# Loading the first batch first, keeping the tensor engine warm, and sampling the scores between projections, in a fused attention kernel

## The chip, the cores and the metric

The kernel runs on one core of a Trainium2 chip. A core has a tensor engine for matrix products (PE in the profile, with its weight loads listed as PEld), a vector engine (DVE), a scalar engine (ACT), a general-purpose engine (POOL) and a synchronising engine (SP) that here only starts transfers. Each engine works through its own list of instructions in order and waits on semaphores for the others. The metric is the device time of one execution in microseconds (us); the smaller the better. The kernel before takes 2685.39 us, the median of three runs that lie between 2684.89 and 2687.76.

## The reference

Four batches of an image of 128 channels and 64 x 64 = 4096 positions go through a group normalisation and an attention over positions with 64-wide queries and keys, then through a causal attention over the same 4096 tokens, then through a recurrent layer. Cut to what matters here:

```python
# layer 0: group norm over groups of 4 channels and all positions, then full attention
xn = _gn(x)                                   # mean and variance of 4 channels x 4096 positions
q = einsum('oc,bcn->bon', Wq, xn) + bq        # 64 wide
k = einsum('oc,bcn->bon', Wk, xn) + bk        # 64 wide
v = einsum('oc,bcn->bon', Wv, xn) + bv        # 128 wide
probs = softmax(einsum('bci,bcj->bij', q, k)) # 4096 x 4096 for each batch
x = x + einsum('bcj,bij->bci', v, probs)
# layer 1: layer norm over channels, causal attention, residual
t = t + causal_attention(_ln_t(t), Wq, Wk, Wv)
# then a layer norm, a product with W, a batch norm over all tokens,
# and a recurrence y = sigmoid(wx_t + y @ V.T) over positions, residual
```

Nothing of the attention of a batch can start before the statistics of that whole batch are known, because the normalised input feeds every projection.

## The kernel before

Only the parts that the change and the prediction touch are shown; `...` marks cuts. `P` is 128, `QT` is 512, `N` is 4096, `NQ` is 8, `B` is 4, `CQ` is 64.

The loads stand first. The input goes into one on-chip tile `X` by eight transfers of half a batch each, started by SP; all weights and biases are started by ACT. The transfers of both engines share a small set of completion semaphores in turn, so a transfer late in the list waits for an earlier one that used the same semaphore, whichever engine started that.

```python
    X = xpool.tile([P, B, N], F32, name="X")
    for b in range(B):
        for h in range(2):
            cols = ts(h, N // 2)
            nc.sync.dma_start(out=X[:, b, cols], in_=x[b, :, cols])        # L91
    def load(src, shape, name):
        t = const.tile(shape, F32, name=name)
        nc.scalar.dma_start(out=t, in_=src)
        return t
    ...
    for h in range(2):
        nc.scalar.dma_start(out=W0k[:, h, :], in_=w0k)
        nc.scalar.dma_start(out=W0q[:, h, :], in_=w0q)
        nc.scalar.dma_start(out=B0k[ds(h * CQ, CQ), :], in_=b0k)
        nc.scalar.dma_start(out=B0q[ds(h * CQ, CQ), :], in_=b0q)
    W0v = load(w0v, [P, C], "W0v")
    ...                                        # B0v, W1q, W1k, W1v, FW, FV, Fgamma, Fbeta
```

Then constants (`ident`, `same`, `ones`, `group`, `mask`, `blocks`). Before any work on the batches, the query and key weights of layer 1 are folded into one matrix:

```python
        for n, w in (("q", W1q), ("k", W1k)):
            pw = ps_m.tile([P, P], F32, tag="m", name=f"pw_{n}")
            nc.tensor.transpose(pw, w, ident)                              # L210
            wt[n] = tmp.tile([P, P], F32, tag="wt", name=f"wt_{n}")
            nc.vector.tensor_copy(wt[n], pw)                               # L212
        pa = ps_m.tile([P, P], F32, tag="m", name="pa")
        nc.tensor.matmul(pa, lhsT=wt["q"], rhs=wt["k"], start=True, stop=True)   # L214
        nc.vector.tensor_scalar(A1, pa, float(C) ** -0.5, None, ALU.mult)        # L216
```

The work on a batch is a set of jobs, each a generator whose steps are put between the steps of the attention. `ps_m` has two buffers (tag "m") and serves all the small products. The group norm scales the weights rather than the input:

```python
        def groupnorm(b):
            for c in range(NQ):
                nc.vector.bn_stats(stats[:, c, :], X[:, b, ts(c, QT)])     # L260
                if c % 2:
                    yield
            nc.vector.bn_aggr(mv, stats...)                                # L264
            nc.tensor.matmul(pg, lhsT=gmat, rhs=mv, ...)                   # L267
            nc.vector.tensor_copy(gmv, pg)
            ...                                     # dev = (mean - group mean) squared
            yield
            nc.tensor.matmul(pd, lhsT=gmat, rhs=dev, ...)                  # L275
            ...                                     # gmv += pd; grs = (var + eps) ** -0.5 on POOL
            yield
            for n, w in (("k", W0k), ("v", W0v), ("q", W0q)):
                nc.vector.tensor_scalar(got[n], src, grs, None, ALU.mult)  # L284
            yield
            for i, n in enumerate("kvq"):
                nc.tensor.matmul(pb[:, i : i + 1], lhsT=got[n], rhs=gmv[:, 0:1], ...)   # L288
            ...                                     # biases bk, bv, bq
            for c in range(NQ):
                feeds[b].append(queue(feed0(b, c)))
                if c == 0:
                    preps[0, b, 0] = queue(prep0(b, 0))
        def feed0(b, c):                            # keys and values of 512 positions
            nc.tensor.matmul(pk, lhsT=gn[b]["k"], rhs=src, ...)            # L308
            nc.scalar.activation(K[0, b][:, ts(c, QT)], pk, AF.Identity, bias=gn[b]["bk"])
            yield
            for j in range(4):
                nc.tensor.matmul(pv[:, j, :], lhsT=src[:, ts(j, P)], rhs=gn[b]["v"], ...)   # L313
            nc.scalar.copy(V[0, b][:, 4 * c : 4 * c + 4, :], pv)
            yield
        def prep0(b, c):                            # queries of 512 positions
            nc.tensor.matmul(pq, lhsT=gn[b]["q"], rhs=X[:, b, ts(c, QT)], ...)   # L319
            nc.scalar.activation(Q[0, b, c], pq, AF.Identity, bias=gn[b]["bq"])
            yield
            if c == 0:
                yield from sample(0, b)
        def sample(layer, b):                       # one shift for all exponentials of the batch
            nc.tensor.matmul(pz, lhsT=K[layer, b][rows, 0:P], rhs=Q[layer, b, 0][rows, :], ...)
            nc.vector.tensor_reduce(m1, pz, AX.X, ALU.max)
            yield
            nc.tensor.transpose(pm, m1, ident)
            nc.vector.tensor_reduce(m2, pm, AX.X, ALU.max)
            yield
            nc.tensor.matmul(px, lhsT=ones[0:1, :], rhs=m2, ...)
            nc.vector.tensor_scalar(t, px, -1.0, SHIFT, ALU.mult, ALU.add)
            yield
```

The attention itself runs over units of 256 keys by 512 queries: `score(i)` makes two score products (tile `ps`), adds the causal mask on the diagonal, and takes the exponential on ACT; `product(i)` multiplies it with the values (tile `av`) and adds it into a running total on DVE. Layer 0 has 8 x 16 units for each batch, layer 1 has 72. The scores of the next unit are issued ahead of the products of this one:

```python
        start_batch(0)                              # queues groupnorm(0)
        score(0)                                    # completes all feeds and the sample first
        for i in range(len(units)):
            if i + 1 < len(units):
                score(i + 1)
            turn()                                  # one step of each of the first two jobs
            product(i)
```

`product` calls `start_batch(b + 1)` at the first unit of the fourth query block of layer 1, so that the group norm of the next batch runs within layer 1 of this one. The order in which each engine finally holds its instructions is not that of the text alone: the recording layer moves an instruction forward where it sees its operands ready. In the kernel before, the 24 `bn_stats` of batches 1 to 3 stand on DVE at the very start of the program, among those of batch 0.

Of the kernel before, what the change touches and what calls it, by code (L numbers as in the profile page):

```python
# [26 lines left out]
F32 = mybir.dt.float32  # L27
AF = mybir.ActivationFunctionType
ALU = mybir.AluOpType
# [3 lines left out]
P = 128  # L33
QT = 512
# [30 lines left out]
def fast(  # L65
# [10 lines left out]
    nc = tc.nc  # L76
    B, C, N = x.shape
    CQ = w0q.shape[1]
    NQ = N // QT
# [4 lines left out]
    const = ctx.enter_context(tc.tile_pool(name="const", bufs=1))  # L84
    xpool = ctx.enter_context(tc.tile_pool(name="xres", bufs=1))

    X = xpool.tile([P, B, N], F32, name="X")
    for b in range(B):
        for h in range(2):
            cols = ts(h, N // 2)  # L90
            nc.sync.dma_start(out=X[:, b, cols], in_=x[b, :, cols])  # L91

    def load(src, shape, name):
        t = const.tile(shape, F32, name=name)
        nc.scalar.dma_start(out=t, in_=src)
        return t


    W0q = const.tile([P, 2, CQ], F32, name="W0q")
    W0k = const.tile([P, 2, CQ], F32, name="W0k")  # L100
    B0q = const.tile([P, 1], F32, name="B0q")
    B0k = const.tile([P, 1], F32, name="B0k")
    for h in range(2):
        nc.scalar.dma_start(out=W0k[:, h, :], in_=w0k)
        nc.scalar.dma_start(out=W0q[:, h, :], in_=w0q)
        nc.scalar.dma_start(out=B0k[ds(h * CQ, CQ), :], in_=b0k)
        nc.scalar.dma_start(out=B0q[ds(h * CQ, CQ), :], in_=b0q)
    W0v = load(w0v, [P, C], "W0v")
    B0v = load(b0v.rearrange("o c -> c o"), [P, 1], "B0v")
    W1q = load(w1q, [P, C], "W1q")  # L110
    W1k = load(w1k, [P, C], "W1k")
    W1v = load(w1v, [P, C], "W1v")
    FW = load(fw, [P, C], "FW")
    FV = load(fv, [P, C], "FV")
    Fgamma = load(fgamma, [P, 1], "Fgamma")
    Fbeta = load(fbeta, [P, 1], "Fbeta")


    ident = const.tile([P, P], F32, name="ident")
    make_identity(nc, ident)  # L120
    same = const.tile([P, R], F32, name="same")
    nc.vector.tensor_reduce(same, ident.rearrange("p (i r) -> p r i", r=R), AX.X, ALU.add)
    ones = const.tile([P, P], F32, name="ones")
    nc.gpsimd.memset(ones, 1.0)
    mhalf = const.tile([P, 4], F32, name="mhalf")
    nc.gpsimd.memset(mhalf, -0.5)
    group = const.tile([P, P // G, G], F32, name="group")
# [1 line left out]
    for base, sign in ((0, 1), (G - 1, -1)):  # L129
        nc.gpsimd.affine_select(  # L130
            out=group, in_=group, pattern=[[-sign * G, P // G], [0, G]], base=base,
# [6 lines left out]
        out=mask, in_=mask, pattern=[[1, P]], base=0,  # L138
# [13 lines left out]
    def rsqrt(dst, src, eps, n):  # L152

        nc.vector.tensor_scalar(dst, src, eps, None, ALU.add)  # L154
        nc.gpsimd.tensor_tensor(dst, dst, mhalf[:, :n], ALU.pow)  # L155
# [39 lines left out]
    with ExitStack() as actx:  # L195
# [3 lines left out]
        tmp = actx.enter_context(tc.tile_pool(name="tmp", bufs=2))  # L199
# [3 lines left out]
        ps_av = actx.enter_context(tc.tile_pool(name="ps_av", bufs=1, space=PSUM))  # L203
        ps_m = actx.enter_context(tc.tile_pool(name="ps_m", bufs=2, space=PSUM))


        wt = {}
        for n, w in (("q", W1q), ("k", W1k)):
            pw = ps_m.tile([P, P], F32, tag="m", name=f"pw_{n}")
            nc.tensor.transpose(pw, w, ident)  # L210
            wt[n] = tmp.tile([P, P], F32, tag="wt", name=f"wt_{n}")
            nc.vector.tensor_copy(wt[n], pw)  # L212
        pa = ps_m.tile([P, P], F32, tag="m", name="pa")
        nc.tensor.matmul(pa, lhsT=wt["q"], rhs=wt["k"], start=True, stop=True)  # L214
        A1 = const.tile([P, P], F32, name="A1")
        nc.vector.tensor_scalar(A1, pa, float(C) ** -0.5, None, ALU.mult)  # L216

        jobs = deque()

        def queue(steps):  # L220
            job = Job(steps)
            jobs.append(job)
            return job
# [8 lines left out]
        norms, ends, preps, feeds = {}, {}, {}, {}  # L232
# [23 lines left out]
        def groupnorm(b):  # L256

            stats = small.tile([P, NQ, 6], F32, tag="stats", name=f"stats_{b}")
            for c in range(NQ):
                nc.vector.bn_stats(stats[:, c, :], X[:, b, ts(c, QT)])  # L260
                if c % 2:
                    yield
            mv = small.tile([P, 2], F32, tag="mv", name=f"mv_{b}")
            nc.vector.bn_aggr(mv, stats.rearrange("p c s -> p (c s)"))  # L264
            gmat = group.rearrange("p a g -> p (a g)")
            pg = ps_m.tile([P, 2], F32, tag="m", name=f"pg_{b}")
            nc.tensor.matmul(pg, lhsT=gmat, rhs=mv, start=True, stop=True)  # L267
            gmv = small.tile([P, 2], F32, tag="gmv", name=f"gmv_{b}")
            nc.vector.tensor_copy(gmv, pg)
            dev = small.tile([P, 1], F32, tag="dev", name=f"dev_{b}")  # L270
            nc.vector.tensor_tensor(dev, mv[:, 0:1], gmv[:, 0:1], ALU.subtract)
            nc.vector.tensor_tensor(dev, dev, dev, ALU.mult)
            yield
            pd = ps_m.tile([P, 1], F32, tag="m", name=f"pd_{b}")
            nc.tensor.matmul(pd, lhsT=gmat, rhs=dev, start=True, stop=True)  # L275
            nc.vector.tensor_tensor(gmv[:, 1:2], pd, gmv[:, 1:2], ALU.add)
            grs = small.tile([P, 1], F32, tag="grs", name=f"grs_{b}")
            rsqrt(grs, gmv[:, 1:2], 1e-5, 1)
            yield
            got = {}  # L280
            for n, w in (("k", W0k), ("v", W0v), ("q", W0q)):
                src = w if n == "v" else w.rearrange("p h o -> p (h o)")
                got[n] = small.tile([P, P], F32, tag=f"w{n}", name=f"w{n}_{b}")
                nc.vector.tensor_scalar(got[n], src, grs, None, ALU.mult)  # L284
            yield
            pb = ps_m.tile([P, 3], F32, tag="m", name=f"pb_{b}")
            for i, n in enumerate("kvq"):
                nc.tensor.matmul(  # L288
                    pb[:, i : i + 1], lhsT=got[n], rhs=gmv[:, 0:1], start=True, stop=True
                )  # L290
            for i, (n, bias) in enumerate((("k", B0k), ("v", B0v), ("q", B0q))):
                got["b" + n] = small.tile([P, 1], F32, tag=f"b{n}", name=f"b{n}_{b}")
                nc.vector.tensor_tensor(got["b" + n], bias, pb[:, i : i + 1], ALU.subtract)
            gn[b] = got
# [5 lines that stand above are left out]
# [99 lines left out]
        for layer, b, c in tiles:  # L399
            n = 2 * (c + 1) if layer else N // (2 * P)  # L400
# [7 lines left out]
        def score(i):  # L408
            layer, b, c, u, n = units[i]
            t = layer, b, c  # L410
            if u == 0:
                if layer == 0 and c == 0:
                    for job in feeds[b]:
                        job.complete()
                if layer == 1:
                    ends[0, b, c].complete()
                    norms[b, c].complete()
                if t not in preps:
                    preps[t] = queue((prep1 if layer else prep0)(b, c))
                preps[t].complete()  # L420
                totals[t] = tot.tile([P, 2, QT], F32, tag="total", name=f"tot_{layer}_{b}_{c}")
            s = totals[t] if u == 0 else sp.tile([P, 2, QT], F32, tag="s", name=f"s_{i}")
            exps[i] = s
            first = [columns(layer, c, u, h) for h in range(2)]
            ps = ps_pair.tile([P, 2, QT], F32, tag="pair", name=f"ps_{i}")
            for h in range(2):
                rows = slice(0, P) if layer else ds(h * CQ, CQ)
                nc.tensor.matmul(  # L428
                    ps[:, h, first[h] :], lhsT=K[layer, b][rows, ts(2 * u + h, P)],
                    rhs=Q[t][rows, first[h] :], start=True, stop=True,  # L430
                )
            if layer and u >= 2 * c:
                for h in range(2):
                    edge = ps[:, h, ds(first[h], P)]
                    nc.vector.tensor_tensor(edge, edge, mask, ALU.add)  # L435
                if u == 0:
                    nc.gpsimd.memset(s[:, 1, : first[1]], 0.0)
            for a in [(slice(None), slice(0, QT))] if first[1] == 0 else [
                (h, slice(first[h], QT)) for h in range(2)
            ]:  # L440
                nc.scalar.activation(s[:, *a], ps[:, *a], AF.Exp, bias=shift[layer, b])  # L441
# [48 lines left out]
        def start_batch(b):  # L490
            feeds[b] = []
            feeds[b].append(queue(groupnorm(b)))

        start_batch(0)
        score(0)
        for i in range(len(units)):
            if i + 1 < len(units):
# [549 lines left out]
```

## Time and profile before

| what | value |
|---|---|
| time, median of 3 | 2685.39 us |
| span of the profiled execution | 2683.1 us |
| tensor engine busy | 97% of the span |
| vector engine busy | 56% |
| scalar engine busy | 42% |
| first half of batch 0 usable on DVE | 6.50 us |
| first matmul of any kind | 15.57 us |
| first key projection | 24.25 us |
| first exponential | 49.28 us |
| first product with the values | 50.45 us |

Times in the table from the fifth row on are starts, counted from the start of the span. To read the profile: the timeline lists merged instructions as start, busy time, engine, source line, operation, output and input tiles, shape and count, and in square brackets the idle time of the engine just before it with what ended it. The chain of waits goes back from the last instruction through whatever released each step, so its shares say which engine the end of the kernel hung on. One product of 128 x 512 values appears as two matmul records, and a record's busy time is modelled, so that times between starts say more than lengths.

### The profile page before, as it was taken

The numbers are of one execution on the slowest core, as the hardware profiler recorded it, in microseconds if no ns is written. First come the engines' busy times: TensorE is split into PE (matmuls) and PEld (weight loads), VectorE is DVE, ScalarE is ACT, GpSimd is POOL, SyncE is SP. The second block draws the span as 40 slices with busy tenths as digits, with TensorE's granted clock in tenths as the row PEclk, the third lists the DMA queues.
The fourth block names the chain that finished last, engine by engine and source line by source line (L and its number), as shares of the span: only waits on it lengthen the run. The fifth ranks groups of instructions, "written<-read, shape, count | busy, mean of one in ns | idle before, by whom it ended". The sixth has DMA issues, their size and how long they took to land.

```text
span 2683.1 us, 25668 instructions
## 1 busy us (share of the span) xinstructions
PE 2598.7 (97%) x9970; PEld 1226.6 (46%) x9970; DVE 1497.6 (56%) x2552; ACT 1118.0 (42%) x1302; POOL 110.9 (4%) x130
## 2 busy tenths in 40 slices
PE   6999999999999999999999999999999999999974
PEld 3444444445444444454444444544544444454443
DVE  4565656544555556553556565654455656555466
ACT  3444443333444444333444444334344444333353
POOL 0000000000000000000000000000000000000005
PEclk9999999999999999999999999999999999999987
DMA  3000000000000000000000000000000000100013
GB/s 133 1 1 1 1 0 12 8 5 4 5 1 1 1 1 5 12 4 9 4 1 1 1 1 1 12 8 4 5 4 1 1 0 1 67 12 8 4 67 127
DMA packets 9234, 35.81 MB, mean 13 GB/s; under 512 B 2192, under 2 KB 2960, under 8 KB 7056
## 3 DMA queue, kind: packets, MB, share of 16 engines
q1 hardware_dynamic: 6912, 33.56, 3.2%
q8 instruction: 80, 1.31, 0.2%
q10 hardware_dynamic: 2192, 0.53, 0.1%
q14 instruction: 50, 0.41, 0.0%
HBM read 17.30 MB, written 16.78 MB: 13 GB/s over the span
## 4 chain that ended last, share of the span: by engine, by line
PE 89%; DVE 7%; ACT 1%; issue 1%; DMA 0%; POOL 0%; ACTq 0%; DVEq 0%; POOLq 0%
PE av L457 47%; PE ps L428 31%; DVE tot L475 2%; DVE pg L545 1%; PE pq L319 1%; ACT s L441 1%; PE pv L313 1%; PE pk L308 1%; PE po L377 1%; PE pq L340 1%; PE pw L389 1%; DVE zt L354 1%; DVE tot L351 1%; DVE part L356 1%; PE pt L161 1%
## 5 line engine op out<-in xcount | busy, mean ns | idle before, releaser
L457 PE MATMUL av<-s,V 64*128 64x512 f32 (+3 forms) x4864 | 1361.9, 588 | 0.0
L441 ACT ACTIVATE s<-ps,shift 128x1024 f32<-128x1024 f32 (+4 forms) x796 | 808.4, 1023 | 1316.2 <-PE ps L428 1174.2
L475 DVE TENSOR_TENSOR tot<-tot,s 128x1024 f32<-128x1024 f32 (+4 forms) x796 | 878.7, 1109 | 855.5 <-ACT s L441 733.0
L428 PE MATMUL ps<-q,K 64*128 64x512 f32 (+4 forms) x3200 | 1029.3, 579 | 0.0
L457 PEld LDWEIGHTS av<-s,V 64*128 64x128 f32 (+1 forms) x4864 | 547.2, 188 | 592.3 <-issue 584.9
L428 PEld LDWEIGHTS ps<-q,K 64*128 64x128 f32 (+1 forms) x3200 | 417.0, 189 | 481.8 <-issue 470.7
L457 PE MATMUL av<-tot,V 64*128 64x512 f32 (+2 forms) x384 | 123.0, 603 | 6.1 <-DVE acc L469 5.8
L441 ACT ACTIVATE tot<-ps,shift 128x1024 f32<-128x1024 f32 (+2 forms) x68 | 71.4, 1057 | 104.3 <-PE ps L428 84.1
L155 POOL TENSOR_TENSOR rstd<-rstd,mhalf 128x4 f32<-128x4 f32 x32 | 32.2, 1007 | 1441.5 <-DVE rstd L154 1441.5
L457 PEld LDWEIGHTS av<-tot,V 64*128 64x128 f32 (+1 forms) x384 | 49.0, 188 | 70.0 <-issue 38.5
L155 POOL TENSOR_TENSOR rstd_f<-rstd_f,mhalf 128x4 f32<-128x4 f32 x32 | 33.4, 1045 | 915.3 <-DVE rstd_f L154 915.3
L543 PE MATMUL pg<-Y,FV 128*128 128x256 f32 x208 | 53.3, 418 | 16.6 <-ACT Y L546 10.0
L435 DVE TENSOR_TENSOR ps<-ps,mask 128x128 f32<-128x128 f32 x128 | 38.0, 297 | 33.8 <-PE ps L428 31.5
L174 DVE TENSOR_SCALAR V<-xt,mv,rstd 128x128 f32<-128x128 f32 x128 | 36.0, 342 | 34.4 <-POOL rstd L155 34.4
L174 DVE TENSOR_SCALAR rows<-xt_f,mv_f,rstd_f 128x128 f32<-128x128 f32 x128 | 36.7, 342 | 31.2 <-POOL rstd_f L155 31.2
L546 ACT ACTIVATE Y<-pg,bias 128x256 f32<-128x256 f32 x104 | 45.8, 474 | 18.5 <-DVE pg L545 17.9
L543 PEld LDWEIGHTS pg<-Y,FV 128*128 128x128 f32 x208 | 36.7, 205 | 34.3 <-ACT Y L546 16.9
L545 DVE SCALAR_TENSOR_TENSOR pg<-X,gain,pg 128x256 f32<-128x256 f32 x108 | 48.2, 491 | 6.9 <-PE pg L543 6.6
L354 DVE STREAM_TRANSPOSE zt<-tot 128x512 f32<-128x512 f32 x64 | 45.5, 710 | 2.1
L378 DVE TENSOR_TENSOR X<-X,po 128x512 f32<-128x512 f32 x32 | 22.0, 688 | 42.7 <-PE po L377 42.7
L351 DVE TENSOR_TENSOR tot<-tot 128x512 f32<-128x512 f32 x64 | 44.3, 692 | 2.2
L365 DVE STREAM_TRANSPOSE rt<-sums 128x512 f32<-128x512 f32 x64 | 45.0, 703 | 0.6
(127 smaller groups left out, 1133.6 us busy)
## 6 DMA issues: line engine op xcount, KB each, us to landing
X<-in_x SPq DMA_DIRECT2D x8, 1024.0 KB, 7.3
D<-X SPq DMA_DIRECT2D x32, 256.0 KB, 2.0
T<-D SPq DMA_DIRECT2D x4, 2048.0 KB, 7.8
out<-T SPq DMA_DIRECT2D x4, 2048.0 KB, 13.5
W0k<-in_w0k ACTq DMA_DIRECT2D x2, 32.0 KB, 5.1
W0q<-in_w0q ACTq DMA_DIRECT2D x2, 32.0 KB, 4.8
W0v<-in_w0v ACTq DMA_DIRECT2D x1, 64.0 KB, 5.3
W1q<-in_w1q ACTq DMA_DIRECT2D x1, 64.0 KB, 7.3
```

Source lines behind the costliest of these rows:

```text
L155: nc.gpsimd.tensor_tensor(dst, dst, mhalf[:, :n], ALU.pow)
L174: nc.vector.tensor_scalar(rows[:, j, :], xt[:, j, :], mv[:, j, 0:1], rstd[:, j : j + 1], ALU.subtract, ALU.mult)
L351: nc.vector.tensor_tensor(both, both, total[:, 1, :], ALU.add)
L354: nc.vector.transpose(zt.rearrange("p j a -> p (j a)"), both)
L365: nc.vector.transpose(rt.rearrange("p (j a) -> p j a", a=R), r.unsqueeze(2).to_broadcast([P, QT // R, R]))
L428: nc.tensor.matmul(ps[:, h, first[h] :], lhsT=K[layer, b][rows, ts(2 * u + h, P)], rhs=Q[t][rows, first[h] :], start=True, stop=True,)
L441: nc.scalar.activation(s[:, *a], ps[:, *a], AF.Exp, bias=shift[layer, b])
L457: nc.tensor.matmul(acc[:, first[h] :], lhsT=V[layer, b][rows, 2 * u + h, :], rhs=s[rows, h, first[h] :], start=u == 0 and h == 0, stop=u = ...
L475: nc.vector.tensor_tensor(total[:, *a], total[:, *a], s[:, *a], ALU.add)
L543: nc.tensor.matmul(ps, lhsT=FV, rhs=last[:, b, :], start=True, stop=True)
L545: nc.vector.scalar_tensor_tensor(pv, wx, gain, pv, ALU.mult, ALU.add)
L546: nc.scalar.activation(y, ps, AF.Sigmoid, bias=bias)
```

## The change

The first part reorders the loads: SP starts batch 0 in four pieces of a quarter before anything else, ACT starts only the three layer-0 weights (the doubled copies of two of them are now made by a broadcast read on DVE), and all other weights and the batches 1 to 3 follow on SP. The second part gives the tensor engine products of a matrix of ones with itself, whose results nobody reads, while the statistics are not there yet: five at the start, one after `pg` and one after `pd`. The third part moves the query projection, the three steps of the score sample and the folding of the layer-1 weights between the key and value projections of batch 0. The fourth part pins the `bn_stats` of batches 1 to 3 to their place in the program (and the first score products after the projections), since their input now arrives later.

```diff
-    for b in range(B):
-        for h in range(2):
-            cols = ts(h, N // 2)
-            nc.sync.dma_start(out=X[:, b, cols], in_=x[b, :, cols])
     def load(src, shape, name):
         t = const.tile(shape, F32, name=name)
+        nc.sync.dma_start(out=t, in_=src)
+        return t
+    for h in range(4):
+        nc.sync.dma_start(out=X[:, 0, ts(h, N // 4)], in_=x[0, :, ts(h, N // 4)])
+    W0k = const.tile([P, CQ], F32, name="W0k")
+    W0v = const.tile([P, C], F32, name="W0v")
+    W0q = const.tile([P, CQ], F32, name="W0q")
+    for t, src in ((W0k, w0k), (W0v, w0v), (W0q, w0q)):
         nc.scalar.dma_start(out=t, in_=src)
-        return t
...
-        nc.scalar.dma_start(out=W0k[:, h, :], in_=w0k)
-        nc.scalar.dma_start(out=W0q[:, h, :], in_=w0q)
-        nc.scalar.dma_start(out=B0k[ds(h * CQ, CQ), :], in_=b0k)
-        nc.scalar.dma_start(out=B0q[ds(h * CQ, CQ), :], in_=b0q)
-    W0v = load(w0v, [P, C], "W0v")
+        nc.sync.dma_start(out=B0k[ds(h * CQ, CQ), :], in_=b0k)
+        nc.sync.dma_start(out=B0q[ds(h * CQ, CQ), :], in_=b0q)
...                                                   (other weights as before, now on sync)
+    for b in range(1, B):
+        nc.sync.dma_start(out=X[:, b, :], in_=x[b])
+    ones = const.tile([P, P], F32, name="ones")       (moved ahead of ident)
+    nc.gpsimd.memset(ones, 1.0)
...
+        def busy(n):
+            for k in range(n):
+                pw = ps_m.tile([P, 4, P], F32, tag="m", name=f"busy_{k}")
+                nc.tensor.matmul(
+                    pw, lhsT=ones, rhs=ones.unsqueeze(1).to_broadcast([P, 4, P]), start=True, stop=True
+                )
+        busy(5)
+        def fold():                                   (the folding of W1q and W1k as a job
+            ...                                        of two steps)
...
-                nc.vector.bn_stats(stats[:, c, :], X[:, b, ts(c, QT)])
+                st = nc.vector.bn_stats(stats[:, c, :], X[:, b, ts(c, QT)])
+                if b:
+                    tc.keep_in_program_order(st)
...
+            if b == 0:
+                busy(1)                               (after pg, and again after pd)
...
-                nc.vector.tensor_scalar(got[n], src, grs, None, ALU.mult)
+                dst = got[n]
+                if n != "v":
+                    dst = dst.rearrange("p (h o) -> p h o", h=2)
+                    w = w.unsqueeze(1).to_broadcast([P, 2, CQ])
+                nc.vector.tensor_scalar(dst, w, grs, None, ALU.mult)
...
+                if i == 0:
+                    tc.keep_in_program_order(mm)      (score products of the first unit)
...
         start_batch(0)
+        feeds[0][0].complete()
+        folded = Job(fold())
+        for c in range(NQ):
+            feeds[0][c + 1].complete()
+            preps[0, 0, 0].step()
+            if c > 2:
+                folded.step()
         score(0)
```

## The prediction

> **What bounds the kernel now.** I read the page first: the shares of the engines and the chain that ended last.
>
> ```profile
> PE 2598.7 (97%) x9970; PEld 1226.6 (46%) x9970; DVE 1497.6 (56%) x2552; ACT 1118.0 (42%) x1302; POOL 110.9 (4%) x130
> PE 89%; DVE 7%; ACT 1%; issue 1%; DMA 0%; POOL 0%; ACTq 0%; DVEq 0%; POOLq 0%
> ```
>
> The tensor engine holds the end for 89% of the span. So only time in which it does nothing, or works slowly, is to be had: 2683.1 - 2598.7 = 84.4 us in all. About 50 of them are the head, the rest the recurrence at the end, which the change doesn't touch. Next I read the timeline of the first 52 us.
>
> ```profile
> 6.50 2.47 DVE L260 BATCH_NORM_STATS2 stats<-X 128x6 f32<-128x512 f32 x4 [6.50 <-DMA X<-in_x]
> ...
> 15.57 0.45 PE L210 MATMUL pw_q<-ident,W1q 128*128 128x128 f32 x1 [15.57 <-DMA W1q<-in_w1q]
> ...
> 16.48 1.27 DVE L260 BATCH_NORM_STATS2 stats<-X 128x6 f32<-128x512 f32 x2
> ...
> 19.68 0.56 PE L267 MATMUL pg<-mv,group 128*128 128x2 f32 x2 [2.28 <-DVE mv L264]
> ...
> 24.25 2.05 PE L308 MATMUL pk<-X,wk 128*128 128x512 f32 x2
> ...
> 32.29 1.02 PE L308 MATMUL pk<-X,wk 128*128 128x512 f32 x2
> ...
> 43.61 1.12 PE L319 MATMUL pq<-X,wq 128*128 128x512 f32 x2
> ...
> 49.28 1.11 ACT L441 ACTIVATE tot<-ps,shift 128x1024 f32<-128x1024 f32 x1 [3.82 <-DVE shift L252]
> ...
> 50.45 1.99 PE L457 MATMUL av<-tot,V 64*128 64x512 f32 x8 [0.34 <-ACT tot L441]
> ```
>
> The reader is to see three delays in a row. DVE stops after four of its eight statistics and goes on at 16.48, although `X` waits for nothing by then: the copies of the transposed layer-1 weights stand before them, and these wait for `W1q`, which lands at 15.5. Then the first key product takes twice the time of the one at 32.29. Then the sample of the scores (43.61 to 49.28) comes after all projections. The queue of SP shows why the loads are late:
>
> ```profile
> SPq L91 <- DMA W1q<-in_w1q: 7.4, 1, 7.4
> SPq L91 <- DMA W0k<-in_w0k: 5.5, 1, 5.5
> ```
>
> The second half of batch 0 isn't even started before 6.5 us, because its semaphore is that of a small weight. Last I looked at the place to which the statistics of the next batches move, the end of a query block in layer 1 (here of batch 0):
>
> ```profile
> 509.65 0.17 DVE L154 TENSOR_SCALAR rstd_f<-mv_f 128x4 f32<-128x4 f32 x1
> ...
> 511.06 1.88 PE L428 MATMUL ps<-q,K 128*128 128x512 f32 x4
> 511.17 0.35 DVE L174 TENSOR_SCALAR rows<-xt_f,mv_f,rstd_f 128x128 f32<-128x128 f32 x1 [0.69 <-POOL rstd_f L155]
> 511.44 0.29 DVE L435 TENSOR_TENSOR ps<-ps,mask 128x128 f32<-128x128 f32 x1
> ...
> 512.78 0.28 PE L267 MATMUL pg<-mv,group 128*128 128x2 f32 x2
> 512.92 0.63 PE L180 MATMUL pb_f<-ident,rows 128*128 128x128 f32 x4
> 513.39 0.82 PE L457 MATMUL av<-s,V 128*128 128x256 f32 x4
> ```
>
> There PE goes from `ps` to `pg` to `pb_f` to `av` without a gap, while DVE is full: its instructions follow each other from 506.95 on but for one wait of 0.69 us for POOL. What is put in front of the mask here is likely to be felt.
>
> [...] the key product takes 2.05 us at 24.25 and 1.02 at 32.29, and the change of pace lies near 31 us, some 7 us after dense work began. The granted clock in the view by stage reads 1.00 there all the same, so that column doesn't show it. [...] the ceiling seen here is about 430 GB/s (20 to 28 us), so what counts is the order.
>
> **Part 1, the loads.** Before, by the transfer view in steps of 1 us (98, 126, 355, 431 and 166 GB/s up to 6 us), 1.18 MB (half a batch and 0.13 MB of weights) were through at about 5.4 us and the half was usable at 6.5. Now another 1.05 MB of batch 0 follows without a break: 1.05 / 0.43 = 2.4 us more, so the last piece is usable at about 8.7 (estimate). The first, at half the volume, at about 4.9. On DVE, eight statistics at 0.62 us a start (2.47 / 4) and the two constants (0.6 us) from 4.9 on end at 10.5; the sum over them takes 0.37, so `pg` starts at about 10.95 instead of 19.68. That is 8.7 us. From `pg` to the first `pk` was 24.25 - 19.68 = 4.57 us; two statistics stood between the small steps on DVE, which now don't (about 1 us less), while the product of ones after `pg` holds `pd` up by about 0.2. I take 3.9: `pk` at 14.85, **9.4 us earlier**.
>
> **Part 2, the products of ones.** A product is two records. Cold, the two of the first `pk` start at 24.25 and 25.25 and the next matmul follows at 26.10, so about 0.85 us each, 1.7 a product; warm, weight loads of `av` follow each other by 0.43 (50.98, 51.41), 0.85 a product. Five of them, from about 1.1 (after the filling of `ones`), end between 7 [...] and 9.6 us (cold throughout). Idle afterwards is at most 3 us, broken by the two single ones. They lie in time in which PE waits, so they cost nothing, and the projections should start warm. Before, `pv` of the first piece started 3.08 us after `pk`, and the second and third `pk` at 4.95 and 8.04 against 1.91 each later.
>
> **Part 3, projections and sample.** Before: from first `pk` to first `av` 50.45 - 24.25 = 26.2 us. Now, all warm: eight rounds at 1.905 us (from 36.0 to 43.61, four rounds in 7.6) = 15.2; the first round waits for the biases, +0.7; between them `pq` 0.95, `pz` 0.95, `pm` with the wait for its maximum 0.8, `px` with the two transposes of the weights and their two-buffer waits 1.35, `pa` 0.8, together 4.85; then one score pair 0.9, one exponential 1.11 and two hand-overs, 2.3. The sum is 23.05, **3.1 us less**. The head should thus be 9.4 + 3.1 = 12.5 us shorter, first `av` at about 37.9.
>
> **Part 4, the statistics of the next batches.** The order of the built programs shows that the 24 pinned `bn_stats` leave the head (where they cost nothing after the change of batch 0) and come two at a time into layer 1, 8 for each of three batches, the last pairs behind the mask of the last diagonal units. The sum `mv` now comes right before `pg` is due. With the times of the block above: a pair (1.27 us) ahead of the layer-norm statistics moves `rstd_f` from 509.65 to about 510.75, and POOL's answer and the second mask by 1.1 to 512.5. The exponential behind it ends its first half at 513.35, where PE is free at 512.78: 0.6 us lost. Then a second pair (1.27), three `rows` (0.85), an addition (0.55) and `mv` (0.37) follow the mask: `mv` at about 515.9. PE, with the last `av` (0.65) and one score product (0.86), is at `pg` at about 514.95: 1.0 us lost. Then `pd` waits for `dev`, which stands behind two additions, a transposition and a reduction: about 0.75 lost. That is 2.4 us a batch, and 3 x 2.4 = **7.2 us given back**. All else (800 units, the recurrence) has the same order on every engine.
>
> The sum is -12.5 + 7.2 = -5.3 us, 2680.1. I take 2679, as slack that I don't see would make the second term smaller rather than larger.
>
> **The rivals.** (a) The statistics cost nothing in the loop: DVE is busy 12.8 of 20 us from 500 to 520, so there is room on average. Then 2673. Against it: the room isn't where the pairs stand, and PE has none at all (20.0 of 20). (b) The transfers don't get faster: in the first 3 us they moved only 0.22 MB, and if four pieces share the engines evenly instead of following each other, DVE starts near 8 and `pg` slips by 2 to 3 us: 2682. (c) PE cools down between the five products and `pk`, the projections start cold, and 3 us come back: 2682. (d) The two-buffer waits among the inserted small products are longer than thought; `sample` then saves nothing: 2682. For none of them does the loss exceed the head, so slower than before needs two or more together.
>
> **Range and chances.** The head gives 10 to 15 us, the loop takes 1 to 9. Together the time lies between 2671 and 2685 eight times in ten. Two per cent are 53.7 us, more than the whole head, so faster by over 2% is out of reach, and nothing here could cost as much: 0.01 each way.
>
> **What would show it.** In the profile after: last statistics of batch 0 done near 10.5 and `pg` near 11; first `pk` near 15 with a length near 1.0, not 2.05; no `pw_q` ahead of `pg`; first `av` near 38. Around 510 (now some 12 us earlier), 1145 and 1780: PE idle before `av`, `pg` or `pd`, with waits on `mv`, `dev` or the exponential, some 2.4 us for each batch. The prediction is wrong if `av` starts before 34 or after 42, or if these three places show no waits.

## The result and the profile after

The changed kernel takes 2676.89 us, the median of four runs from 2676.43 to 2678.88, against 2685.47 before: a ratio of 0.9968, 95% interval 0.9951 to 0.9985. The span of the profiled execution goes from 2683.1 to 2674.8 us. The gain is 8.6 us, 0.3%.

The page of the changed kernel shows the same bound:

```profile
PE 2604.0 (97%) x9984; PEld 1222.2 (46%) x9984; DVE 1498.0 (56%) x2552; ACT 1118.9 (42%) x1302; POOL 111.0 (4%) x130
PE 88%; DVE 9%; ACT 1%; issue 1%; DMA 0%; POOL 0%; SPq 0%; DVEq 0%; POOLq 0%; ACTq 0%
```

PE's busy time has *grown* by 5.3 us with the products of ones: idle time was filled with work that nobody reads, so a share of busy time can rise while the kernel gets shorter. The timeline of the head of the changed kernel (start, busy time, engine, line, operation, tiles, shape, count, and idle time before it with what ended that):

```profile
5.25 1.28 DVE L274 BATCH_NORM_STATS2 stats<-X 128x6 f32<-128x512 f32 x2 [5.25 <-DMA X<-in_x]
...
9.89 1.28 DVE L274 BATCH_NORM_STATS2 stats<-X 128x6 f32<-128x512 f32 x2
...
11.72 0.35 PE L283 MATMUL pg<-mv,group 128*128 128x2 f32 x2 [3.90 <-DVE mv L280]
...
13.38 0.42 PE L293 MATMUL pd<-dev,group 128*128 128x1 f32 x2
...
16.01 1.10 PE L331 MATMUL pk<-X,wk 128*128 128x512 f32 x2
...
38.01 1.11 ACT L466 ACTIVATE tot<-ps,shift 128x1024 f32<-128x1024 f32 x1 [0.48 <-PE ps L451]
...
39.17 1.99 PE L482 MATMUL av<-tot,V 64*128 64x512 f32 x8 [0.36 <-ACT tot L466]
```

`pg` starts at 11.72 instead of 19.68, the first key product is 1.10 us long instead of 2.05, and the first product with the values starts at 39.17 instead of 50.45: **11.28 us won in the head**. Only 8.3 of them are left in the span. The place in layer 1 where the next batch's statistics now stand shows where the rest goes (same columns, block of batch 0):

```profile
493.97 1.67 PE L451 MATMUL ps<-q,K 128*128 128x512 f32 x4
...
499.03 0.16 DVE L155 TENSOR_SCALAR rstd_f<-mv_f 128x4 f32<-128x4 f32 x1
...
500.64 0.30 DVE L460 TENSOR_TENSOR ps<-ps,mask 128x128 f32<-128x128 f32 x1
500.84 1.28 DVE L274 BATCH_NORM_STATS2 stats<-X 128x6 f32<-128x512 f32 x2
...
501.58 0.92 PE L482 MATMUL av<-s,V 128*128 128x256 f32 x4
...
503.26 0.36 DVE L280 BATCH_NORM_AGGREGATE mv<-stats 128x2 f32<-128x48 f32 x1
...
503.69 0.38 PE L283 MATMUL pg<-mv,group 128*128 128x2 f32 x2 [0.32 <-DVE mv L280]
...
506.42 0.38 PE L293 MATMUL pd<-dev,group 128*128 128x1 f32 x2
...
507.60 1.88 PE L451 MATMUL ps<-q,K 128*128 128x512 f32 x4
```

The same two score products before:

```profile
505.25 1.67 PE L428 MATMUL ps<-q,K 128*128 128x512 f32 x4
...
517.70 1.88 PE L428 MATMUL ps<-q,K 128*128 128x512 f32 x4
```

Ahead of this block the score product of 505.25 before is at 493.97, 11.28 earlier. Behind it that of 517.70 is at 507.60, 10.10 earlier. So the block costs **1.18 us**. The waits of PE in the loop name it; the columns are total, times, longest:

```profile
PE pg L283 <- DVE mv L280: 1.0, 3, 0.3
```

This row isn't there before, and its three times are the three blocks (503.69, 1140.42, 1777.15). It holds under a third of the cost: the rest is time that PE lost before `av` and `pd` and in broken hand-overs, which no row carries. The last `av` of the loop is at 2558.25 after and 2565.99 before, 7.74 apart, and 11.28 - 3 x 1.18 = 7.74.

### The profile page after: what moved, and what is told of

Read it like the earlier page. It is cut to its first block, busy times and chain, and to the rows that moved or that the text cites. A ratio compares the mean times of both kernels' runs of the same rounds, so it can differ in the third digit from the quotient of the medians.

```text
span 2674.8 us, 25695 instructions
## 1 busy us (share of the span) xinstructions
PE 2604.0 (97%) x9984; PEld 1222.2 (46%) x9984; DVE 1498.0 (56%) x2552; ACT 1118.9 (42%) x1302; POOL 111.0 (4%) x130
## 4 chain that ended last, share of the span: by engine, by line
PE 88%; DVE 9%; ACT 1%; issue 1%; DMA 0%; POOL 0%; SPq 0%; DVEq 0%; POOLq 0%; ACTq 0%
PE av L482 47%; PE ps L451 31%; DVE tot L500 2%; DVE pg L577 1%; PE pq L342 1%; ACT s L466 1%; PE pv L336 1%; PE po L400 1%; PE pk L331 1%; PE pq L363 1%; PE pw L412 1%; DVE zt L377 1%; DVE tot L374 1%; DVE part L379 1%; PE pt L162 1%
```

## The experiments

One number tells the head from the loop in every kernel: the start of the first `av` is the head, and from there to the last `po` product is the loop.

| kernel | first pk, us (length) | first av, us | loop, us | time, median (lowest to highest) |
|---|---|---|---|---|
| before | 24.25 (2.05) | 50.45 | 2523.2 | 2685.47 (2684.89 to 2687.76) |
| changed | 16.01 (1.10) | 39.17 | 2526.8 | 2676.89 (2676.43 to 2678.88) |
| no_ones | 15.46 (2.05) | 41.85 | 2527.0 | 2679.39 (2678.68 to 2680.69) |
| single_ones | 16.49 (1.11) | 39.60 | 2526.8 | 2677.44 (2676.67 to 2679.14) |
| nine_ones | 15.09 (1.10) | 38.25 | 2526.7 | 2675.56 (2675.35 to 2675.83) |
| sample_last | 15.53 (2.06) | 44.88 | 2526.8 | 2681.93 (2677.70 to 2686.19) |
| nine_late | 15.06 (1.10) | 39.87 | 2527.7 | 2677.92 (2676.97 to 2681.30) |
| unpinned | 15.76 (2.06) | 42.27 | 2523.2 | 2676.38 (2674.52 to 2677.48) |
| stats_early | 16.88 (2.05) | 43.43 | 2523.2 | 2676.13 (2672.10 to 2677.38) |
| nine_unpinned | 15.10 (1.10) | 38.48 | 2523.1 | 2672.68 (2672.15 to 2672.78) |
| old_loads | 20.55 (2.05) | 45.33 | 2526.7 | 2681.52 (2679.62 to 2683.16) |
| pin_only | 23.35 (2.06) | 49.52 | 2526.7 | 2687.98 (2686.32 to 2689.85) |
| nine_early_consts | 14.69 (1.10) | 37.85 | 2523.2 | 2671.74 (2671.24 to 2672.34) |

The theory to test was that of the prediction: loads, full rate and interleaving shorten the head, and the pinned statistics give some of it back in the loop.

**The pin, alone and taken away.** *pin_only* is the kernel before with nothing but the pin:

```diff
-                nc.vector.bn_stats(stats[:, c, :], X[:, b, ts(c, QT)])
+                st = nc.vector.bn_stats(stats[:, c, :], X[:, b, ts(c, QT)])
+                if b:
+                    tc.keep_in_program_order(st)
```

> The kernel before with one thing from the change, the pin on the statistics of batches 1 to 3. Theory: the loop pays 1.2 us at each of three places as in the changed kernel, 3.5 us; the head wins up to 1 us, as the statistics of later batches no longer stand between the small steps from pg to pk: 2.5 to 3.5 us longer than before, 2688. Rival: the waits in the loop of the changed kernel come from its other changes (the order around pg); then the time is that of before or up to 1 us shorter.

Measured: 1.0009 of before, 95% interval 1.0000 to 1.0017, 2.7 us longer than before on the same chip (2687.98 against 2685.24). The head wins 0.93 us (50.45 to 49.52), the loop grows by 3.5, and the row of waits comes with the pin:

```profile
PE pg L269 <- DVE mv L266: 1.0, 3, 0.3
```

So it is the pin, and not the rest of the change. *unpinned* is the changed kernel without those two added lines:

> The changed kernel without the pin on the statistics of batches 1 to 3; in its built order they stand in the head again, four of them ahead of the shift, the rest up to the first addition. Theory (they cost 1.2 us of PE each time at three places in layer 1, and DVE is free in the head): the head loses at most 1.5 us, because batch 1 has landed by about 19 us; the waits before pg, pd and av near 504, 1140 and 1777 vanish: 3.5 - 1.5 = 2 us shorter than the changed kernel. Rival (the pin is needed): DVE stands still for the late batches in front of the shift, the first exponential slips by 4 us or more, and the time is longer than that of the changed kernel by 0.5 us or more.

Measured: 0.9965 (0.9952 to 0.9979), 2676.38. The loop is back at 2523.2, as the theory has it, but the head got *longer* by 3.1 us, and neither side had said why: its first `pk` is 2.06 us long. *stats_early* moves the statistics away from the diagonal units and leaves the head alone:

```diff
+            if layer == 1 and b + 1 < B and c in (2, 3) and u < 4:
+                ...                       # tile of statistics of batch b + 1, once
+                k = 4 * (c - 2) + u
+                tc.keep_in_program_order(
+                    nc.vector.bn_stats(early[b + 1][:, k, :], X[:, b + 1, ts(k, QT)])
+                )
```

> The changed kernel with the eight statistics of the next batch put one at a time behind the first four units of the third and of the fourth query block of layer 1, away from the diagonal units. Theory: their cost in the loop is that of the place alone: first av stays at 39.2, the waits of PE before av, pg and pd (0.08 + 0.5 + 0.3 us, and 0.1 for each hand-over broken) vanish at all three places, 3 x 1.18 = 3.5 us shorter than the changed kernel. Rival: DVE has no slack in layer 1 wherever they stand, the same wait turns up at another place, and the time stays within 1 us of the changed kernel.

Measured: 0.9958 (0.9944 to 0.9972), 2676.13, and two of its five runs at 2672.10 and 2672.86. The loop is back at 2523.2, all of the 3.5 us, so the place was the cost and not the work. But here too the profiled execution has a first `pk` at half rate and a first `av` at 43.43. Neither of these two changes touches the projections, and yet both traces have them at half rate.

**The products of ones.** *no_ones* takes `busy(5)` and both `busy(1)` out:

> The changed kernel without any product of ones. Theory: the seven products keep the array at full rate, so without them the first projections run at half rate for about 7 us, which costs half of that, 3.5 us; the product behind pg, which kept pd waiting, is gone, which gives 0.7 back: first pk near 15.3 with a length near 2 us, first av near 42.0 instead of 39.2, time about 2.8 us longer than the changed kernel. Rival A: the projections wait for ACT and the two buffers anyway, so a cold array is hidden: first av 38.5 to 39.2. Rival B: the five early products are no use, since the array cools again in the 4.5 us between them and pg; then the result is the same as in the theory, and only the two single ones matter.

Measured: 0.9977 (0.9968 to 0.9987), 2679.39, 2.5 us longer than the changed kernel, `pg` at 11.82, `pk` at 15.46 and cold, `av` at 41.85, all as the theory had it; rival A is out. But it is *steadier* than the kernels with five products of ones at the start (2 us between the lowest and the highest of ten runs, where *sample_last* has 8.5 in twelve). The weight loads tell the rate of the array, as they take 0.34 us where a product takes twice its time (half rate, "cold") and 0.19 at full rate ("warm"). In the changed kernel:

```profile
4.63 0.34 PEld L211 LDWEIGHTS busy<-ones 128*128 128x128 f32 x1 [0.52 <-issue]
...
5.95 0.19 PEld L211 LDWEIGHTS busy<-ones 128*128 128x128 f32 x1 [0.24 <-issue]
...
13.38 0.34 PEld L293 LDWEIGHTS pd<-dev,group 128*128 128x128 f32 x1 [0.38 <-issue]
...
16.52 0.19 PEld L311 LDWEIGHTS pb<-gmv,wq 128*128 128x128 f32 x1 [0.24 <-issue]
```

and in *stats_early*, with the same instructions on PE up to there:

```profile
4.44 0.19 PEld L211 LDWEIGHTS busy<-ones 128*128 128x128 f32 x1 [0.33 <-issue]
...
13.18 0.34 PEld L296 LDWEIGHTS pd<-dev,group 128*128 128x128 f32 x1 [0.52 <-DVE dev L291]
...
18.73 0.34 PEld L314 LDWEIGHTS pb<-gmv,wq 128*128 128x128 f32 x1 [0.52 <-issue]
```

Both warm up, both are cold again at `pd`, and only one is warm in time for `pk`. Ahead of `pg` PE had stood without work for 3.90 us in the changed kernel and for 4.59 in *stats_early*. The trace lists the clock that the array was granted, and the view by stage shows it. Each of its lines has a stretch and its length, the busy time of PE, PEld, DVE, ACT and POOL, then the granted clock, and last the share and the rate of the transfers. The changed kernel:

```profile
5.53:12.36 6.83, 2.93 (x9) 1.27 (x8) 5.84 (x13) 0.00 (x0) 0.00 (x0) 1.00 0.67 224
12.36:15.77 3.41, 3.41 (x8) 1.59 (x7) 1.25 (x7) 0.00 (x0) 0.56 (x1) 0.50 0.77 202
15.77:39.17 23.40, 21.47 (x104) 13.24 (x104) 2.20 (x9) 12.04 (x19) 0.00 (x0) 1.00 0.56 241
```

and *stats_early*:

```profile
4.24:11.07 6.83, 2.94 (x7) 0.95 (x5) 5.40 (x10) 0.00 (x0) 0.00 (x0) 1.00 0.75 270
11.07:24.72 13.65, 12.57 (x28) 7.33 (x29) 2.27 (x13) 1.96 (x3) 0.56 (x1) 0.50 0.92 351
24.72:43.43 18.71, 17.17 (x86) 10.75 (x84) 1.91 (x6) 10.08 (x16) 0.00 (x0) 1.00 0.21 91
```

The reader is to see the 0.50, and the lengths 6.83, 3.41, 6.83 and 13.65: two, one, two and four times 3.41 us. The changed kernel's own `pd` is cold too, and its array is back at full rate at 15.77, just 0.24 us before `pk`: the five early products had been lost, and its warm projections were partly luck. The other traces with five products agree. In *unpinned*, *sample_last* and *old_loads* the clock is full from 6.29, 6.92 and 4.94 us, falls to 0.50 after 6.83 us in each, and stays there for 10.24, 10.24 and 13.65 us: all of these lengths are multiples of 3.41 us too. The moment of the first rise is not the same in any two of the five, although their products of ones all start at 1.05 or 1.06 us; over the nine traces with products that start so early it lies anywhere from 4.02 to 6.92 us. What sets that moment was not shown.

The executions without a trace carry their mean granted clock, and it sorts the scatter. In *stats_early* it is 0.990 and 0.989 for the two runs below 2673 us and 0.987 to 0.988 for the other three. In *unpinned* all five have 0.987 to 0.988. In *sample_last* it goes from 0.990 at 2677.70 us down to 0.985 at 2686.19, and of the changed kernel's four runs the longest alone, 2678.88, has 0.988 and not 0.990. The traced executions of *stats_early*, *unpinned* and *sample_last*, cold in the head, are among the low ones (0.987, 0.987, 0.988). As far as this mean tells, the medians thus mix warm and cold heads, and for *unpinned* and *stats_early* the loop, not the total, tells what the statistics cost. In all five traces the clock fell during or within 2 us after the stretch of 3.30 to 7.48 us in which PE had no work ahead of `pg`. If that stretch is the cause, products until `pg` make the head steady, which can be tested. *nine_ones* is `busy(9)` for `busy(5)`:

> The changed kernel with nine products of ones at the start instead of five. The four traces with five products show the array reach full rate at 4.4 to 7.0 us, a different moment in each, and idle for 4 to 5 us before pg at 11.7; after that the first pk is at full rate in one trace (1.10 us) and at half rate in three (2.05). Theory: [...] nine products last until 10.5 to 12.1 us, [...] pk is at full rate in every execution: first pk 1.1 us long, first av 39.0 to 39.6, and the times scatter by under 1.5 us, near 2676.5, where the changed kernel's reach 2678.9. Rival: the three cold traces differ from the warm one for another reason (the order of instructions): then pk is at full rate here with five or with nine, and the time equals the changed kernel's 2676.9; or the rate falls between the single products all the same, and pk is 2.05 us long.

Measured: 0.9961 (0.9948 to 0.9975), 2675.56, and the five runs lie within 0.5 us of each other.

```profile
6.91 0.19 PEld L211 LDWEIGHTS busy<-ones 128*128 128x128 f32 x1 [0.24 <-issue]
...
15.60 0.19 PEld L311 LDWEIGHTS pb<-gmv,wq 128*128 128x128 f32 x1 [0.24 <-issue]
```

No load from 6.91 to `pk` is slow, though this execution warmed late, and the granted clock is 1.00 from 6.62 us through to 2563. `pd` is at 12.93 instead of 13.38, since the single product ahead of it runs at full rate, and `pk` at 15.09. *single_ones* keeps only the two `busy(1)`:

> The changed kernel without the five early products, but with the two single ones behind pg and pd. Theory [...] pk is at half rate; pd still waits for the product behind pg: first av 42 to 43.5, 2679 to 2680.5, like the kernel without any products of ones (2679.4) or up to 1 us longer. Rival: the two single ones alone carry the effect: first pk 1.1 us long and 2676.9 or below.

Measured: 0.9972 (0.9961 to 0.9983), 2677.44, `pd` at 13.97 and cold, but `pk` at 16.49 and 1.11 us long, `av` at 39.60. The theory's half about `pk` failed: the two single products mostly do carry the effect. In its trace the first entry of the granted clock, to full, stands at 15.38 us, 3.3 us after the first of them starts and ahead of `pk`. That is rival B of *no_ones*: little is left for the five early ones, and what they add (0.55 us between the medians) isn't clear of the scatter of either.

**Interleaving.** *sample_last* puts the sample after all projections:

```diff
         for c in range(NQ):
             feeds[0][c + 1].complete()
-            preps[0, 0, 0].step()
             if c > 2:
                 folded.step()
+        preps[0, 0, 0].complete()
```

> The changed kernel with the query projection and the three steps of the sample put after all eight key and value projections (the folding of the layer-1 weights stays between them). Theory: the interleaving hides the chain of q, maximum, transposition, maximum, broadcast, about 7.6 us from pq to av, at the price of about 2.9 us between the projections: first av at 16.0 + 0.7 + 15.2 + 1.7 + 7.6 = 41.2 instead of 39.2, time 2.0 us longer than the changed kernel. Rival: the two-buffer waits of the inserted products eat all of it; then first av stays within 0.5 us of 39.2.

Measured: 0.9986 (0.9977 to 0.9994), 2681.93, from 2677.70 to 2686.19. It is inconclusive by itself: its first `pk` was cold, and the clock fell a second time, from 41.06 to 44.47 us, so that it measures several things. *nine_late* is the same with nine products of ones:

> Nine products of ones (first pk then starts at 15.1 us at full rate, first av at 38.25 with the interleaving), but query projection and sample after all key and value projections: the test of the interleaving with the state of the array held fixed, which the earlier run without that could not give (its first pk was at half rate). Theory: 15.1 + 0.7 + 15.2 + 1.7 + 7.6 = 40.3, so 2.0 us later and longer than nine products with the interleaving (2675.56): 2677.6. Rival: the two-buffer waits eat the gain: within 0.5 us of 2675.56.

Measured: 0.9974 (0.9964 to 0.9983), 2677.92, 2.4 us longer than *nine_ones*, with `pk` at 15.06 and warm in both. The tail that the interleaving hides, in *nine_late*:

```profile
32.45 1.12 PE L342 MATMUL pq<-X,wq 128*128 128x512 f32 x2
34.35 1.12 PE L252 MATMUL pz<-q,K 64*128 64x512 f32 x2 [0.78 <-ACT q L344]
36.26 0.27 PE L259 MATMUL pm<-ident,m 128*1 128x128 f32 x1 [0.79 <-DVE m L256]
36.90 0.38 PE L264 MATMUL px<-m,ones 1*128 1x1 f32 x2 [0.37 <-DVE m L261]
```

`av` itself is only 1.6 us later than in *nine_ones*; the last `po` is 2.6 us later (2567.59 against 2564.97). The other 1.0 us is a further cost of the tail: after PE's three waits in it, of 0.78, 0.79 and 0.37 us, the granted clock falls to 0.50 once more.

```profile
38.16:41.57 3.41, 3.41 (x10) 1.33 (x8) 0.00 (x0) 2.23 (x2) 0.00 (x0) 0.50 0.00 0
```

From the first `av` to the next score product it takes 2.57 us here and 1.82 in *nine_ones*. So of the 2.4 us between the medians at most 1.6 are the chain that the interleaving hides, and the rest is put down to the 0.50, an estimate: 0.75 of the 1.0 us lie between these two starts. Two of the ten runs lost more, 2680.88 and 2681.30 us at a mean clock of 0.988 and 0.987; no trace shows where, so nine products are not shown to be safe in every kernel.

**The loads.** *old_loads* is the changed kernel with the loads of before (`X` in halves, weights on ACT, doubled copies):

> The changed kernel with the loads as they were (X in halves on SP with their waits, all weights on ACT, doubled copies). Theory: the second half of batch 0 lands 5 to 6 us later, because its start waits for a small weight; but the folding of the layer-1 weights no longer stands before the statistics on DVE, so pg is at 15 to 17 instead of 11.7 (and 19.7 before), first av at 43 to 45 with the array at full rate, 46 to 48 at half rate: 4 to 8 us longer than the changed kernel. Rival: the folding alone held DVE up, and the transfers were in time: then pg is below 13 and the time within 1.5 us of the changed kernel.

Measured: 0.9984 (0.9977 to 0.9990), 2681.52, 4.6 us longer than the changed kernel. `pg` is at 15.01, and `pk` is cold (the clock is 0.50 from 11.77 to 25.42), so that the 4.6 us are not the loads alone. The queue of SP waits as before, and DVE for the second half:

```profile
SPq L91 <- DMA W0k<-in_w0k: 5.4, 1, 5.4
```
```profile
11.98 2.47 DVE L273 BATCH_NORM_STATS2 stats<-X 128x6 f32<-128x512 f32 x4 [2.63 <-DMA X<-in_x]
```

So of the 7.96 us by which `pg` came earlier, 15.01 - 11.72 = 3.3 are the loads, and 19.68 - 15.01 = 4.7 come from the folding of the layer-1 weights having left DVE's front. The split holds in this order of taking apart; the new loads with the folding left in front were not run.

**A version that beats both.** *nine_unpinned* takes the pin off with the array kept warm:

> Nine products of ones, and the statistics of batches 1 to 3 without the pin. In the trace of the unpinned kernel with a cold array the way from first pk to first av took 26.5 us, as in the other cold trace with pinned ones moved elsewhere (26.55), so the statistics in the head cost nothing. Theory: first av at 38.3, no waits at the three places of the loop: 3.5 us below 2675.56, 2672.0. Rival: with the array at full rate the sample comes some 4 us sooner, when batch 1 may not have landed (it is started at 12.3 us), so DVE stands in front of the shift: first av at 39.5 or later, 2673 to 2674.

Measured: 0.9953 (0.9939 to 0.9967), 2672.68. The statistics in the head cost 0.2 us (`av` at 38.48):

```profile
24.05 1.86 DVE L274 BATCH_NORM_STATS2 stats<-X 128x6 f32<-128x512 f32 x3
26.69 0.16 DVE L266 TENSOR_SCALAR shift<-px 128x1 f32<-128x1 f32 x1 [0.78 <-PE px L264]
```

DVE even idles for 0.78 us before the shift, and no wait is for a late batch: the rival that the pin is needed fell. *nine_early_consts* joins *nine_ones*, *stats_early* and the two constants made first:

```diff
+    tc.keep_in_program_order(
         nc.vector.tensor_reduce(same, ...)
+    )
...                                         (the same for blocks and for bn_stats of batch 0)
```

> Three mends to the changed kernel at once: nine products of ones, the statistics of the next batches one at a time in the third and fourth query blocks of layer 1, and the two constants that DVE makes (0.5 us between the statistics of batch 0) pinned to the front, where DVE waits for the first piece. Theory: pg 0.5 us earlier at 11.2, first av at 38.6 in every execution, no waits in the loop: 3.5 + 0.5 us below the changed kernel's warm executions (2676.5), 2672.5. Rival: the array still cools in some executions, or the ninth product delays pg: 2674 to 2677.

Measured: 0.9948 (0.9934 to 0.9961), 2671.74, runs from 2671.24 to 2672.34, `pg` at 11.38 and `av` at 37.85, and none of the three waits in the loop. This is 5.2 us below the changed kernel and 13.7 below before.

## Why the prediction was right, and where its steps were off

The mechanism was right: a shorter head, part of it given back at three places of the loop. The range held the time (2671 to 2685; 2676.9 measured, 2679 predicted). That the number came so near is in part luck: the errors of the two terms had opposite signs, and the traced execution was just warm in time. The terms of the sum:

- **Where PE idles.** The prediction put about 50 of the 84.4 idle us into the head and the rest into the recurrence. It is the other way round: up to the first `av` PE is busy for 27.75 of 50.45 us, so 22.7 are idle there, and 47.7 after the loop. Nothing was worked out from this, as the terms below come from starts.

```profile
0.00:50.45 50.45, 27.75 (x109) 17.42 (x110) 23.88 (x54) 13.31 (x20) 2.94 (x14) 1.00 0.48 177
```

- **Loads, `pg` 8.7 us earlier: 7.96 measured.** The first piece is usable at 5.25, not 4.9; DVE's eight statistics and the two constants end at 11.17, not 10.5; the hand-overs around `mv` take another 0.1. The larger error was in the cause. The step gave all of it to the transfers, while *old_loads* shows 3.3 us for them and 4.7 for the folding, which the prediction had itself seen standing in front of DVE and then not counted apart.
- **`pg` to `pk`, 3.9: 4.29 measured.** The product of ones between `pg` and `pd` was taken as 0.85 us, warm. It ran in part at half rate and held `pd` until 13.38; with a warm array (*nine_ones*) the way takes 15.09 - 11.78 = 3.31.
- **Products of ones, "cost nothing, and the projections should start warm".** This step failed as put. Idle time after the five was to be at most 3 us, though the prediction's own times, 7 for their end and 10.95 for `pg`, are 3.95 apart; the 7 was the author's estimate and rested on a warm-up that no trace of before showed (there it is 7.67 us from the first `pk` to the rise of the clock). It was 3.90 in the changed kernel and 3.30 to 7.48 in the other four traces with five products, the array cooled in all five of them, and it was warm again at `pk` in one. Rival (c) was thus true of some executions, and the first `av` moves by up to 4 us with it, in *stats_early* to 43.43, past the 42 that the prediction had set as a sign of being wrong. The view by stage, which the prediction set aside because it reads 1.00 in the kernel before, shows the cooling in all five: 0.50 for 3.41 us in the changed kernel and for 10.24 to 13.65 us in the others.
- **Projections and sample, 26.2 to 23.05: 23.16 measured.** Right in size. Cold to full rate is 26.39 (*no_ones*, 41.85 - 15.46) against 23.16, so 3.23; the interleaving is worth 24.81 (*nine_late*, 39.87 - 15.06) - 23.16 = 1.65 up to `av`. Together that is more than the 26.20 - 23.16 = 3.04 won, so the moved folding takes about 1.8 back, an estimate from these differences.
- **The statistics in the loop, 2.4 us a batch: 1.18 measured, 3.5 in all instead of 7.2.** The mechanism was right (*pin_only*, *unpinned* and *stats_early* all turn the same 3.5 us on and off); each wait was mis-sized. From the block above, against the same starts of before less 11.28: before `av` 0.08 us instead of 0.6, because an addition of 0.55 us had moved from in front of the mask to behind it and `rstd_f` slipped by 0.66 instead of 1.1; before `pg` 0.49 instead of 1.0; before `pd` 0.3 instead of 0.75. Three broken hand-overs of 0.1 us each weren't counted. The prediction's picture of DVE as full from 506.95 on but for one wait also left out a wait of 0.42 us for ACT at 508.00. Rival (a), no cost at all, fell.

The sum -12.5 + 7.2 was -11.28 + 3.54 = -7.74: both terms were too large, the second by more. The span is 0.6 us shorter than that still, in the recurrence after the last batch; no run here settles why, and it is within the scatter of the times.

## What to carry to other kernels

A pin that keeps work in the order of the text also keeps it at the place of the text: look which instructions of its engine it lands in front of there. Here eight statistics on a DVE that is busy for 56% of the span cost a PE that is busy for 97% of it 1.18 us at each of three places. Look also how close idle-time products reach up to the real work. In the five traces here with a gap of 3.30 to 7.48 us ahead of `pg` the clock fell to 0.50, and only one was back at 1.00 for `pk`: executions become unequal, and a single profile can show the lucky one. With products until `pg` the five runs of *nine_ones* lie within 0.5 us. To judge a change of a few us, split the time at one event that all kernels share; the loop lengths above tell a 3.5 us effect that the total times hide in scatter.

## What the runs showed of the hardware that was not expected

In the heads of these kernels the granted clock of the array took two values, 1.00 and 0.50, and every stretch between two of its changes was a whole number of steps of 3.41 us, from one to ten (34.13 us from 4.02 to 38.16 in *nine_late*). Equal products of ones from 1.05 or 1.06 us on brought it to 1.00 at 4.02 to 6.92 us in nine executions. Projections from a cold start took longer: 7.06 us from the first `pk` in *no_ones* (15.46 to 22.52) and 7.67 before (24.25 to 31.92); no run settles why. In *sample_last* PE stood for 3.30 us, from 8.51 to 11.81, and the clock fell at 13.75, although work had begun again. In *nine_late* it stayed at 1.00 over a wait of 1.25 us (10.50 to 11.75), and fell at 38.16 behind three waits of 1.94 us together, between 33.57 and 36.90.

In these traces the granted clock tells the rate only from its first entry on. The trace of the kernel before has none ahead of 31.92 us and that of *no_ones* none ahead of 22.52, and the view reads 1.00 up to there although the first `pk` takes twice its time. Before the first entry, the 0.34 against 0.19 us of a 128 x 128 weight load tells the two rates apart.
